# Tile pools that wait for the users of their own bytes: a four-layer perceiver in F32

## The chip, the cores and the metric

The kernel runs on one core of a Trainium2 chip (trn2). The metric is device time in microseconds for one launch. Five engines of the core have their own instruction streams: TensorE (PE in the profile, with its weight loads as PEld), VectorE (DVE), ScalarE (ACT), GpSimd (POOL) and SyncE (SP), which here mainly issues DMAs. [...]

## The reference

A perceiver of depth 4 on 128 latent tokens of width 256 (`x`), with a context of 12544 rows of width 192. Each layer adds three things to `x`, one after the other: cross-attention from the latents to the context, self-attention among the latents, and a feed-forward part with 8 experts.

- Cross-attention: `q = norm(x) Wq`, `k = ctx Wk`, `v = ctx Wv`, softmax over the context, then `Wo`. Layers 0 to 2 have 16 heads of 16; layer 1 also guards against keys that are not finite (it computes a mean of the values to put in their place); layer 3 has 16 heads of 64 and low-rank additions to its weights, the output's being `o_down` and `o_up`.
- Self-attention differs by layer: with a gate and scales (0), differential with lambda vectors and a norm (1), rotary (2), causal (3).
- Feed-forward: a router gives each token its experts; experts are gated or plain MLPs of inner width 1024.

All arithmetic that matters is F32.

## The kernel before

**Stages.** `run` (L1653) goes through the four layers in order; a layer is one cross-attention (`l0_xattn`, `xattn_biased` twice, `l3_xattn`), one self-attention (`l0_attn` to `l3_attn`) and one feed-forward (`l0_ffn` to `l3_ffn`). In the profile the cross-attentions take 0-564, 693-1217, 1372-1900 and 2010-2973 us; what lies between them are the joints, in which the self-attention and experts run (L0 564-686, L1 1217-1364, L2 1900-2007, L3 2974 to the end).

**Cross-attention.** `attend_twice` (L493, layers 0 to 2) reads the context twice in blocks of 512 rows: once for the highest score, once for exp and the weighted sum. The line numbers that come up are L102 (keys and values from the context), L538/L539 (scores and their maxima), L575/L581/L595 (scores again, exp, weighted values). At its end the accumulator is copied to `oT` (L649), transposed into `pair` (L652) and divided into `o`. `attend_once` (L660, layer 3) keeps scores in SBUF and goes over the context once. The queries lie in one tile `qz` with two halves, written by two DVE instructions (L295).

**Joints.** After layer 1's cross-attention `nan_guard` checks the keys' sums: `wide` and `many` are small constants made by DVE, then three products on TensorE, `ps<-wq,xT`, `ps<-wk,wide` with `ps<-row,many` (the row is the bias `bk`), and one with `wv`. After layer 3's cross-attention the output projection of `l3_xattn` opens the pool `out3` and a weights pool, loads `wo` and `od` (`o_down`), transposes `o3`, and multiplies: 16 matmuls with `od`, 16 with `wo`, then the row `bo` and the low-rank part `low`. `l3_attn` follows with `w_q`, `w_k`, `w_v`, `w_o`. A `softmax` (L466) is: DVE maximum and subtraction, ACT exp (L472), DVE sum, reciprocal and product.

**Loads.** `load_w` (L304, DMA at L311), `load_kv` (L322, L324), `load_row` (L335), `all_rows` (L341, a row broadcast to 128 partitions) and `load_b1` (L1597) put their DMAs on SP's queue, which issues in program order: a load that waits holds all loads behind it. The early context blocks of the next layer go over GpSimd's queue (L390, L392).

**Pools.** All tiles come from tile pools. Pools are stacked: a pool that is closed gives its range of SBUF (or its PSUM banks) back, and the next pool opened takes the same range. `const`, `wsmall`, `rows`, `xres`, `act`, `stat`, `ahead`, `broad` stay open all along; the pools of a stage (`x0`, `twice`, `a1`, `f3`, `once`, `out3`, `weights` and so on) open and close around it, and the PSUM pools are closed and opened anew by `psum` (L237) at each change of stage. Between a new pool's tile and what used the range before it, the framework puts semaphore waits; the scheduling of instructions on the engines' queues is otherwise the order of the program text.

## Time and profile before

| what | value |
|---|---|
| median of 3 runs | 3115.3 us (3112.16 to 3123.14) |
| profiled execution, its own time | 3119.43 us |
| its span | 3116.6 us |
| mean granted TensorE clock | 0.968 |
| busy: PE, DVE, ACT, POOL | 2966.8, 1955.4, 1469.2, 295.3 us |
| bytes read from HBM | 241.65 MB, 78 GB/s over the span |

The profile is of one execution; engines' busy times add up over instructions that overlap other engines' work. The chain is the sequence of work that ended last, followed back through what released each step. A timeline line gives start, length, engine, source line, operation with its output and inputs, and in brackets the engine's idle time before it and what ended that. The idle of an engine that is not the bottleneck costs nothing. Where TensorE works in 50 us stretches, it is busy for 35.0 us of 650-700, 43.4 of 1200-1250, 39.5 of 2950-3000 and 36.5 of 3000-3050; in the cross-attentions it is nearly full.

### The profile page before, as it was taken

How to read it: one execution, taken by the hardware profiler on the slowest of the kernel's cores; microseconds unless marked ns; L12 is line 12 of the kernel's file. 1: busy time of each engine (PE TensorE's matmuls, PEld its weight loads, DVE VectorE, ACT ScalarE, POOL GpSimd, SP SyncE). 2: the span in 40 equal slices, each digit the busy share in tenths (PEclk: the TensorE clock that was granted, in tenths of full speed). 3: DMA queues.
4: the chain of work that ended last, by engine and by line, in shares of the span. 5: the costliest groups of instructions: out<-in, count | busy, mean ns of one | idle time of the engine just before them, and what ended most of it. 6: DMA issues, size and time to landing. Idle time of an engine off the chain costs nothing.

```text
span 3116.6 us, 78239 instructions
## 1 busy us (share of the span) xinstructions
PE 2966.8 (95%) x35065; PEld 2248.6 (72%) x35065; DVE 1955.4 (63%) x2300; ACT 1469.2 (47%) x1869; POOL 295.3 (9%) x349
## 2 busy tenths in 40 slices
PE   8999999879999999899999999899999999999979
PEld 6677667535576576665676576489889889889858
DVE  7802850439997897769208603467777777777844
ACT  1187149411383185211572275256556565556511
POOL 6601630212000000110000001000000000000000
PEclk9999999989999998999999999899999999999979
DMA  5100210552002102441102106332323222322436
GB/s 134 52 18 26 72 39 3 188 204 58 25 3 62 53 14 75 126 130 50 31 13 70 46 3 203 118 86 81 87 78 87 80 85 81 87 82 84 121 109 204
DMA packets 165254, 246.83 MB, mean 79 GB/s; under 512 B 19853, under 2 KB 106831, under 8 KB 164920
## 3 DMA queue, kind: packets, MB, share of 16 engines
q1 hardware_dynamic: 160200, 227.67, 24.1%
q0 software_dynamic: 4608, 14.16, 1.4%
q8 instruction: 275, 4.51, 0.6%
q14 instruction: 59, 0.48, 0.1%
q10 hardware_dynamic: 112, 0.01, 0.0%
HBM read 241.65 MB, written 0.13 MB: 78 GB/s over the span
## 4 chain that ended last, share of the span: by engine, by line
PE 78%; DVE 11%; ACT 5%; issue 3%; DMA 2%; POOL 1%; SPq 0%; DVEq 0%; ACTq 0%; POOLq 0%
PE pair L102 20%; PE pair L538 9%; PE v L102 8%; PE pair L575 7%; PE pair L595 6%; PE sc L701 6%; PE acc L743 6%; PE ps L275 4%; DVE parts L539 4%; ACT e L581 3%; PE pair L567 2%; PE kv L102 2%; DVE e L289 2%; PE acc L275 2%; PE ps L1532 1%
## 5 line engine op out<-in xcount | busy, mean ns | idle before, releaser
L539 DVE TENSOR_REDUCE parts<-pair 128x2 f32<-128x1024 f32 x600 | 678.9, 1196 | 103.8 <-PE pair L538 103.7
L102 PE MATMUL pair<-ctxA,wk 128*128 128x256 f32 x1236 | 328.7, 399 | 1.4 <-ACT kT L193 1.1
L649 DVE COPY oT<-pair 128x256 f32<-128x256 f32 x6 | 2.5, 424 | 505.5 <-PE pair L595 505.5
L102 PEld LDWEIGHTS pair<-ctxA,wk 128*128 128x128 f32 x1236 | 217.2, 190 | 140.0 <-DVE parts L539 96.0
L538 PE MATMUL pair<-kT,qz 32*128 32x512 f32 (+1 forms) x1632 | 277.7, 612 | 9.3 <-DVE parts L539 8.9
L703 ACT COPY kept<-sc 128x1024 f32<-128x1024 f32 (+1 forms) x135 | 136.2, 1009 | 260.7 <-PE sc L701 260.6
L286 DVE TENSOR_TENSOR top<-top,kept 128x1024 f32<-128x1024 f32 (+2 forms) x145 | 169.1, 1169 | 135.0 <-ACT kept L703 133.8
L575 PE MATMUL pair<-qz,kT 32*128 32x256 f32 x3168 | 251.6, 374 | 0.0
L581 ACT ACTIVATE e<-pair,maskcol 128x512 f32<-128x512 f32 x392 | 237.0, 688 | 16.1 <-PE pair L575 14.9
L289 DVE SCALAR_TENSOR_TENSOR e<-pair,floor 128x1024 f32<-128x1024 f32 x196 | 230.3, 1218 | 7.1 <-PE pair L575 1.1
L587 ACT ACTIVATE e<-e 128x1024 f32<-128x1024 f32 x196 | 207.2, 1057 | 38.0 <-DVE e L289 30.4
L583 ACT ACTIVATE e<-pair 128x1024 f32<-128x1024 f32 x196 | 189.9, 1021 | 60.3 <-PE pair L575 60.3
L595 PE MATMUL pair<-e,v 128*17 128x128 f32 x6336 | 212.3, 274 | 2.0 <-ACT e L587 1.0
L575 PEld LDWEIGHTS pair<-qz,kT 32*128 32x128 f32 x3168 | 205.3, 187 | 10.8
L132 ACT ACTIVATE kT<-pair,bk 128x512 f32<-128x512 f32 (+1 forms) x68 | 45.9, 674 | 347.4 <-PE pair L102 323.5
L595 PEld LDWEIGHTS pair<-e,v 128*17 128x17 f32 x6336 | 156.6, 97 | 67.1 <-issue 42.5
L701 PE MATMUL sc<-qz,kT 64*128 64x128 f32 x2816 | 197.8, 279 | 0.0
L102 PEld LDWEIGHTS v<-wv,ctxA 128*128 128x128 f32 x1568 | 189.8, 192 | 6.4 <-issue 1.9
L567 PE MATMUL pair<-low,ones 32*128 32x512 bf16 x1176 | 190.4, 389 | 3.6 <-DVE low L558 3.1
L102 PE MATMUL v<-wv,ctxA 128*128 128x128 f32 x1568 | 193.1, 276 | 0.0
L102 PE MATMUL pair<-ctxB,wk 64*128 64x256 f32 x1236 | 188.3, 398 | 0.0
L701 PEld LDWEIGHTS sc<-qz,kT 64*128 64x128 f32 x2816 | 171.6, 187 | 13.0 <-issue 1.3
(425 smaller groups left out, 4866.2 us busy)
## 6 DMA issues: line engine op xcount, KB each, us to landing
ctxA<-in_ctxA SPq DMA_DIRECT2D x324, 256.0 KB
ctxB<-in_ctxB SPq DMA_DIRECT2D x339, 128.0 KB
w<-in_L_ffn_W SPq DMA_DIRECT2D x32, 1024.0 KB
ctxA<-in_ctxA POOLq DMA_DIRECT2D x36, 256.0 KB, 3.3
w<-in_L_ffn_w_gateT SPq DMA_DIRECT2D x8, 1024.0 KB
wu<-in_L_ffn_w_upT SPq DMA_DIRECT2D x8, 1024.0 KB
w<-in_L_ffn_w_downT SPq DMA_DIRECT2D x8, 1024.0 KB
w<-in_L_ffn_w1T SPq DMA_DIRECT2D x8, 1024.0 KB
```

The costliest lines, as they stand in the source:

```text
L102: self.nc.tensor.matmul(out, a, b, start=start and not low, stop=low == 1, skip_group_check=True)
L275: self.nc.tensor.matmul(out, lhsT, rhs, start=(i == 0), stop=(i == n - 1))
L289: self.nc.vector.scalar_tensor_tensor(out, a, s, b, op0, op1, **kw)
L538: nc.tensor.matmul(x[:, i, :n], qz[r, g, s, :], keys.kT(b)[r, :n], start=not masked, stop=True)
L539: nc.vector.tensor_reduce(parts[:, s, 2 * half : 2 * half + 2, b], x[:, :, :n], AX.X, ALU.max)
L567: nc.tensor.matmul(x[:, i, :], self.ones16[r, :], m[r, :], start=True, stop=False, skip_group_check=True)
L575: nc.tensor.matmul(at, kT[r, k], q, start=False, stop=True, skip_group_check=True)
L581: nc.scalar.activation(to[:, :, part], x[:, :, part], AF.Exp, bias=self.mask_col[:, c + j : c + j + 1])
L583: nc.scalar.activation(to, x, AF.Exp)
L587: nc.scalar.activation(to, to, AF.Exp)
L595: nc.tensor.matmul(acc[32 * t : 32 * t + 17, s, :P], v[:, c % 4 + j, 2 * t + s, :], es[t // 2][:, t % 2, j, s, :], start=c + j == 0, stop= ...
L701: nc.tensor.matmul(x[:, t, c : c + P], kT[r, c : c + P], qz[r, g, :], start=True, stop=True)
```

## The change

Every `tile_pool` call, at 21 places, gets `reuse_waits="tile"`. Before, the first use of a tile of a newly opened pool waits until all users of the released pools whose range the new pool lies on are done. After, a tile waits only for the users of the bytes on which it lies itself. Tiles keep their addresses, and the program's arithmetic, transfers and order of statements stay as they are. The diff is the same edit at each place; these carry the stages named above:

```diff
@@ Net.__init__ (const, wsmall, rows, xres, act, stat, ahead, broad)
-        pool = lambda name, bufs, **kw: ctx.enter_context(tc.tile_pool(name=name, bufs=bufs, **kw))
+        pool = lambda name, bufs, **kw: ctx.enter_context(tc.tile_pool(name=name, bufs=bufs, **kw, reuse_waits="tile"))
...
@@ psum: all PSUM pools
-            setattr(self, name, self.banks.enter_context(self.tc.tile_pool(name=name, bufs=bufs, space=PSUM)))
+            setattr(self, name, self.banks.enter_context(self.tc.tile_pool(name=name, bufs=bufs, space=PSUM, reuse_waits="tile")))
...
@@ large_weights
-        self.wp = self.tc.tile_pool(name="weights", bufs=bufs)
+        self.wp = self.tc.tile_pool(name="weights", bufs=bufs, reuse_waits="tile")
...
@@ attend_twice ("twice"), attend_once ("once") likewise
-        with self.tc.tile_pool(name="twice", bufs=2) as pool:
+        with self.tc.tile_pool(name="twice", bufs=2, reuse_waits="tile") as pool:
...
@@ xattn_biased (its own pool, "layer3", "guard"), l0_xattn ("x0", "layer3") likewise
-                with self.tc.tile_pool(name="guard", bufs=1) as own:
+                with self.tc.tile_pool(name="guard", bufs=1, reuse_waits="tile") as own:
...
@@ l3_xattn ("x3" and "out3")
-            with self.tc.tile_pool(name="out3", bufs=1) as last, self.large_weights() as self.wp:
+            with self.tc.tile_pool(name="out3", bufs=1, reuse_waits="tile") as last, self.large_weights() as self.wp:
...
@@ l0_attn to l3_attn ("a0" to "a3"), l0_ffn to l3_ffn ("f0" to "f3"), run ("narrow") likewise
-        with self.tc.tile_pool(name="a1", bufs=2) as pool:
+        with self.tc.tile_pool(name="a1", bufs=2, reuse_waits="tile") as pool:
```

More of the change, by code (lines that the diff above doesn't have):

```diff
@@ L666, in attend_once @@
         self.psum(ppr=1, pv=1, psc=1, pacc=1, pps=1)
-        with self.tc.tile_pool(name="once", bufs=2) as pool:
+        with self.tc.tile_pool(name="once", bufs=2, reuse_waits="tile") as pool:
             self.queue = self.nc.sync
@@ L862, in l0_xattn @@
         nc, d = self.nc, self.d
-        with self.tc.tile_pool(name="x0", bufs=2) as pool:
+        with self.tc.tile_pool(name="x0", bufs=2, reuse_waits="tile") as pool:
             wq = self.load_w(d["L0_xattn_Wq"], 2, D, "wq")
@@ L878, in l0_xattn @@
             o = self.ap.tile([P, D], F32, tag="o", name="o")
-            with self.tc.tile_pool(name="layer3", bufs=1) as other:
+            with self.tc.tile_pool(name="layer3", bufs=1, reuse_waits="tile") as other:
                 self.attend_twice(o, qz, keys, masked=True, between=self.prepare_l3(other))
@@ L897, in xattn_biased @@
         nc, d = self.nc, self.d
-        with self.tc.tile_pool(name=name, bufs=2) as pool:
+        with self.tc.tile_pool(name=name, bufs=2, reuse_waits="tile") as pool:
             xT = self.normed(x)
@@ L913, in xattn_biased @@
             else:
-                with self.tc.tile_pool(name="layer3", bufs=1) as other:
+                with self.tc.tile_pool(name="layer3", bufs=1, reuse_waits="tile") as other:
                     self.attend_twice(o, qz, keys, between=self.last_tokens_l3(other))
@@ L1062, in l3_xattn @@
         dims, rate = H * 64, self.rate
-        with self.tc.tile_pool(name="x3", bufs=2) as pool:
+        with self.tc.tile_pool(name="x3", bufs=2, reuse_waits="tile") as pool:
             xT = self.normed(x)
@@ L1136, in l0_attn @@
         nc, d = self.nc, self.d
-        with self.tc.tile_pool(name="a0", bufs=2) as pool:
+        with self.tc.tile_pool(name="a0", bufs=2, reuse_waits="tile") as pool:
             wide = pool.tile([P, 2 * P], F32, tag="wide", name="wide", bufs=1)
@@ L1316, in l2_attn @@
         nc, d = self.nc, self.d
-        with self.tc.tile_pool(name="a2", bufs=2) as pool:
+        with self.tc.tile_pool(name="a2", bufs=2, reuse_waits="tile") as pool:
             w = [self.load_w(d[f"L2_attn_{k}T"], 2, D, k) for k in ("wq", "wk", "wv", "wo")]
@@ L1347, in l3_attn @@
         dims = H * 64
-        with self.tc.tile_pool(name="a3", bufs=2) as pool:
+        with self.tc.tile_pool(name="a3", bufs=2, reuse_waits="tile") as pool:
             causal = pool.tile([P, P], F32, tag="causal", name="causal", bufs=1)
@@ L1601, in l0_ffn @@
         d = self.d
-        with self.tc.tile_pool(name="f0", bufs=2) as pool:
+        with self.tc.tile_pool(name="f0", bufs=2, reuse_waits="tile") as pool:
             xn = self.layernorm(x)
@@ L1609, in l1_ffn @@
         d = self.d
-        with self.tc.tile_pool(name="f1", bufs=2) as pool:
+        with self.tc.tile_pool(name="f1", bufs=2, reuse_waits="tile") as pool:
             xT = self.normed(x)
@@ L1625, in l2_ffn @@
         nc, d = self.nc, self.d
-        with self.tc.tile_pool(name="f2", bufs=2) as pool:
+        with self.tc.tile_pool(name="f2", bufs=2, reuse_waits="tile") as pool:
             b1 = pool.tile([NE, FF], F32, tag="b1", name="b1", bufs=1)
@@ L1637, in l3_ffn @@
         d = self.d
-        with self.tc.tile_pool(name="f3", bufs=2) as pool:
+        with self.tc.tile_pool(name="f3", bufs=2, reuse_waits="tile") as pool:
             xT = self.normed(x)
@@ L1668, in run @@
         made = []
-        narrow = self.tc.tile_pool(name="narrow", bufs=1)
+        narrow = self.tc.tile_pool(name="narrow", bufs=1, reuse_waits="tile")
         self.lw = narrow.__enter__()
```

## The prediction

> **What bounds the kernel now.** I read the page first: busy rows, then the chain that ended last.

> ```profile
> PE 2966.8 (95%) x35065; PEld 2248.6 (72%) x35065; DVE 1955.4 (63%) x2300; ACT 1469.2 (47%) x1869; POOL 295.3 (9%) x349
> ...
> PE 78%; DVE 11%; ACT 5%; issue 3%; DMA 2%; POOL 1%; SPq 0%; DVEq 0%; ACTq 0%; POOLq 0%
> ```

> TensorE is busy for 2966.8 of 3116.6 us, so all its idle time is 150 us, and no change that only removes waits can win more than that (plus whatever the clock gives back). Most of the chain is TensorE's own work. The idle time sits in the joints between stages (550-700, 1200-1300, 1900-2050, 2950-3050 us), which is also where pools are opened and closed. So the prediction is a list of joints, not a percentage.

> Next I read whom the SP queue waits for, because SP issues nearly every DMA, in program order. These waits look spectacular:

> ```profile
> SPq L1320 <- PE pair L652: 159.1, 1, 159.1
> SPq L341 <- DVE oT L649: 137.0, 1, 137.0
> SPq L311 <- PE pair L652: 129.1, 1, 129.1
> ```

> Three loads (L2 attention's `turns`, L1 attention's `norm`, L0 attention's `wqkv`) stand for 425 us in all, each held by the last user of a pool that has just closed. That is exactly the kind of wait that the change shortens. But SP is not on the chain (0%), so a shorter wait is worth only what somebody downstream loses to the late load. I read that from the timeline, joint by joint:

> ```profile
> 693.17 1.24 PE L538 MATMUL pair<-kv,qz 32*128 32x512 f32 x4 [0.79 <-DVE qz L295]
> ...
> 1218.02 1.10 PE L275 MATMUL ps<-wq,xT 128*128 128x256 f32 x4 [0.82 <-DVE many L936]
> ...
> 1219.77 0.25 SPq L335 DMA_DIRECT2D row<-in_L_xattn_bk  x1
> 1223.15 1.19 PE L275 MATMUL ps<-row,many 1*128 1x256 f32 x2 [2.35 <-DVE dot L286]
> ...
> 1244.07 1.28 ACT L472 ACT_TABLE_LOAD   x1
> 1250.10 0.63 ACT L472 ACTIVATE e<-e 128x512 f32<-128x512 f32 x1 [4.74 <-DVE e L286]
> 1256.75 0.42 DVE L281 COPY eT<-tr 128x256 f32<-128x256 f32 x1 [1.27 <-PE tr L1245]
> ...
> 2973.82 0.38 SPq L311 DMA_DIRECT2D wo<-in_L_xattn_Wo  x1
> 2979.57 1.65 PE L275 MATMUL ps<-wo,oT 128*128 128x256 f32 x3 [1.47 <-DMA wo<-in_L_xattn_Wo]
> 2985.85 0.25 SPq L335 DMA_DIRECT2D row<-in_L_ffn_b  x1
> 2986.33 0.38 SPq L311 DMA_DIRECT2D w_q<-in_L_attn_w_qT  x1
> 2991.48 0.76 PE L275 MATMUL ps<-xT,w_q 128*128 128x128 f32 x2 [2.53 <-DMA w_q<-in_L_attn_w_qT]
> ```

> The bracket is the engine's idle time before the line, with what ended it. These brackets of 0.8 to 2.5 us, not the 425 us, are the size of the prize.

> **The change, part by part.** Every tile keeps its place and every engine keeps its instruction order: PE 6329, DVE 1183, ACT 947, POOL 250 and SP 710 entries in the same sequence. No transfer and no arithmetic is added. Only wait operations differ (PE 3969 to 3961, DVE 2516 to 2499, ACT 2229 to 2226, SP 1831 to 1832, POOL 498 to 506). Most are gone because a tile lies on bytes that were free long ago; a few sit on another instruction of the same engine. A moved DMA passes nothing on SP or POOL: it can only go out as early as its predecessor.

> *Joints where TensorE itself was held.* At 693.17 and 1371.96 (the first scores of L1 and L2) TensorE had ended its own work 0.79 us earlier and waited for the second of two `qz` writes; now the first one, 2 us older, suffices. That is 2 x 0.7. At 1218.02 it waited 0.82 for the guard's memset of `many`, although `wq` and `xT` were there: 0.7. At 18 us and 564 us the same thing is worth 0.2 and 0.1. Sum 2.4.

> *The L1 guard's row (1219.77).* The freed `norm` load and the two lambda rows behind it leave SP at about 1172 instead of 1217, 45 us early. The loads behind them (`wq`, row `bk`, `wk`) keep their waits on TensorE, so they don't move, but row `bk` no longer queues behind three broadcasts. It was issued at 1219.77 and landed at 1223.01, 3.24 us; TensorE stood for 2.35 us before it (the bracket names `dot`, done at the same moment). With an empty queue what would it take? Other one-row loads of this trace land in about 1.4 us[...]. By the row, the stall shrinks to 0.5 and 1.9 is won; [...] if the queue was not the cause, 0. I take 1.3, since `wq` (256 KB) goes out 0.6 ahead of it in either kernel [...].

> *The L3 output projection (2973.82).* `wo` was held by the last write of `o3` and landed 5.7 us later, so TensorE, done with its own 16 `od` matmuls at 2978.10, stood for 1.47 us. Its bytes are now free at 2953.07 and SP's last load ahead of it leaves at 2958.3: it lands near 2964, ten microseconds before its use. The whole 1.47 goes; next in line is `low` (DVE, at 2978.14), which is used only by the last two matmuls. [...] I looked at the clock over its own grid of 3.41 us:

> ```profile
> 2973.21:2976.63 3.42, 2.62 (x12) 1.97 (x13) 1.18 (x3) 1.87 (x2) 0.00 (x0) 0.50 0.40 108
> 2976.63:2980.04 3.41, 1.94 (x8) 1.34 (x7) 0.34 (x1) 0.00 (x0) 0.00 (x0) 0.50 0.57 199
> 2980.04:2983.45 3.41, 3.41 (x9) 2.69 (x9) 0.00 (x0) 0.00 (x0) 0.00 (x0) 0.50 0.00 0
> 2983.45:2986.87 3.42, 2.80 (x12) 1.83 (x11) 0.55 (x2) 0.00 (x0) 0.49 (x2) 1.00 0.00 0
> ...
> 1232.50:1235.90 3.40, 3.40 (x13) 2.40 (x12) 1.61 (x6) 0.20 (x1) 0.00 (x0) 0.50 0.99 367
> 1235.90:1239.30 3.40, 2.88 (x15) 2.09 (x16) 0.57 (x2) 1.16 (x2) 1.07 (x2) 0.50 0.99 345
> ```

> (Stretch, length, then busy time of PE, PEld, DVE, ACT, POOL, and the granted clock.) The clock is 0.50 until the stretch 2980.04-2983.45 has been busy throughout, and 1.00 after it. [...] By that rule, once the idle 1.47 is gone the window before is full, the clock rises at 2980.04, and the 1.95 us of cold work left there takes half: 0.97 more. But the row 1232.50 speaks against the rule: 3.40 us busy, and the next stretch is still at 0.50. I take half, 0.5, with 0 and 1.0 as ends.

> *The next stall in the same chain (2986.33).* `w_q` loses its own wait (2973.74 instead of 2986.26), which alone would remove up to 2.1 of the 2.53 us bracket. It is behind L3 feed-forward's row `b2` on SP, though, and that one still waits for the `bo` matmul (2985.83) to release a row buffer. So `w_q` leaves only 0.24 earlier relative to its surroundings: 0.2. The bracket at 2991.48 stays.

> *Waits that appear.* Two ACT table loads of 1.28 us (L472 at 1244.07 and at 1916.87) ran while ACT idled; the wait for DVE now sits on the table load and no longer on the `exp` after it, so each `exp` starts 1.28 later (1250.10 to about 1251.4; 1920.90 to about 1922.2). Behind each are DVE's reduction and normalisation, then the transposes. The trace bounds the price: 2 x 1.28 = 2.6 if nothing absorbs it, 0 if DVE's own gaps do (1.27 before `eT` at 1256.75, 1.04 at 1925.21). The gaps are nearly as long as the shift: 0.2. Another such move (L1470 at 1297.35) meets an ACT that is busy anyway.

> *Costed at nothing.* `wqkv` of L0 attention goes out 3.9 earlier (560.06), but lands 2.5 before its use and is paced by `xT` (569.95). `bv` at 669 and 1364, `turns` (used 11 us later, and `w1` behind it on SP keeps its wait until 1901.56), `qu` (TensorE busy until 2011.02), both `b1` loads, POOL's memsets for `v`, `before` and `causal` (the last waited 1020.7 us): each is needed well after it was already there. If that cover were gone, each would cost under 0.5.

> *Sum.* 2.4 + 1.3 + 1.5 + 0.5 + 0.2 - 0.2 = 5.7 us off the profiled execution, which took 3119.4 us (span 3116.6, 2.8 around it). It stands 4.1 above the median of 3115.3; I take the gain off the median: 3109.6. The ends of the terms give 1 to 8.

> **The rivals.** *More than the brackets (30%).* The granted clock averages 0.968; at levels 0.5 and 1 that is 3116.6 x 0.032 x 2, some 199 us at half speed. The stretch 1222.2-1242.7 is one block of it, TensorE busy there for 17.6 of 20.5 us. It went cold after 1218.8-1222.2, in which TensorE was busy for only 2.0 of 3.4 us, partly by the two stalls that go. If it stays warm, up to half of 17.6 could go, but DVE and the expert weights pace that stretch too, so 3 to 6: 3104 to 3107, with another window or two elsewhere 3100. Against it: TensorE's next stalls there are not touched.

> *Nothing (12%).* The bytes are free but each load's next obstacle (its predecessor on SP, its row buffer) is as late as the old one, as for `w_q`; or the tiles lie on the last-used bytes after all. Only the 0.7s remain: 3113 to 3116.

> *Slower (7%): the clock's phase.* All work after 1218 slides by 2 to 5 us over a grid of 3.41 us that doesn't slide with it. [...] From four more cold windows than now (6.8) the gain is eaten; seven cost 11.9 and end at 3121. For it: dozens of windows lie in the joints. Against: the sliding warms as many as it cools, and less idle time makes windows fuller.

> **How the numbers follow.** Forecast 51%, 3109.6, its own range 3105 to 3114. About 0.3% (9.3 us) is what a measurement can tell from no change: 3106. The forecast lies on the near side; a fifth of its chance lies beyond, with most of the "more" case: faster 0.36. Slower keeps 0.06, since part of that rival ends within 9.3 us. The same: 0.58. The range leaves out a tenth on either side: 3099 to 3117.

> **What would show it.** Right: brackets under 0.2 at the first scores of L1 and L2 and at the guard's first product; `norm` issued near 1172; `wo` issued near 2958 and no DMA bracket at its matmul; row `b2` still just ahead of `w_q`, with 2 us or more idle before `w_q`; the two table loads directly ahead of their `exp`. Wrong: `w_q` leaving ten microseconds early; the clock at 1.00 through 1222-1243; a new bracket over 1 us in front of a TensorE line where none stands now; a shift of `exp` that is still there at the end of L1 or L2 attention.

## The result and the profile after

The changed kernel took 3109.7 us (median of 6 executions, 3103.8 to 3111.4), the kernel before 3123.6 us beside it (6 executions): a ratio of 0.996, 95% interval 0.9941 to 0.998. A later repetition (11 executions against 25) gave 3112.1 and 3121.1, ratio 0.9974, interval 0.9966 to 0.9983. So the change is worth 8 to 12 us. The forecast named 3109.6 us and a gain of 5.7. That the time agrees to 0.1 us is luck: the kernel before ran 8 us slower beside it than the median of 3115.3 from which the gain was taken (6 us slower in the later repetition). The gain itself is one and a half to two times the forecast.

The page of the changed kernel, busy rows and the chain that ended last:

```profile
PE 2958.3 (95%) x35065; PEld 2247.1 (72%) x35065; DVE 1954.4 (63%) x2300; ACT 1470.4 (47%) x1869; POOL 296.2 (10%) x349
...
PE 80%; DVE 11%; ACT 5%; issue 2%; DMA 1%; POOL 1%; SPq 0%; DVEq 0%; ACTq 0%; POOLq 0%
```

The span fell by 14.5 us (3116.6 to 3102.1), TensorE's busy time by 8.5, although every matmul is still there. The mean granted clock is 0.973 where it was 0.968; that is the first trace of the part that the forecast had missed. This profile is of the fastest of the six executions, though. The repetition's profile has a span of 3111.5 us and TensorE busy for 2966.4, hardly less than before, so what one profile says of the clock has to be set against many executions, as is done below.

SP's waits, whom it waited for, with total, number and longest:

```profile
SPq L1320 <- PE pair L575: 155.4, 1, 155.4
SPq L311 <- PE pair L575: 125.1, 1, 125.1
...
SPq L341 <- PE pair L595: 93.4, 1, 93.4
```

Two of the three spectacular waits are hardly shorter: 159.1 and 129.1 became 155.4 and 125.1. The third, `norm`, fell from 137.0 to 93.4. They end on an earlier matmul of the same cross-attention. Nobody on the chain needed those loads; `norm` matters only for the small load that stood behind it in the queue, row `bk`.

The timeline at the places that the prediction showed:

```profile
690.40 1.23 PE L538 MATMUL pair<-kv,qz 32*128 32x512 f32 x3
...
1169.93 0.33 SPq L341 DMA_DIRECT2D norm<-in_L_attn_norm_w  x1
...
1215.65 1.03 PE L275 MATMUL ps<-wq,xT 128*128 128x256 f32 x4
...
1217.34 0.24 SPq L335 DMA_DIRECT2D row<-in_L_xattn_bk  x1
1219.15 0.67 PE L275 MATMUL ps<-row,many 1*128 1x256 f32 x2 [0.78 <-DMA row<-in_L_xattn_bk]
...
1244.52 1.28 ACT L472 ACT_TABLE_LOAD   x1 [5.61 <-DVE e L286]
1245.81 0.63 ACT L472 ACTIVATE e<-e 128x512 f32<-128x512 f32 x1
1251.61 0.42 DVE L281 COPY eT<-tr 128x256 f32<-128x256 f32 x1 [0.82 <-PE tr L1245]
...
2946.89 0.43 SPq L311 DMA_DIRECT2D wo<-in_L_xattn_Wo  x1
2963.68 3.62 PE L275 MATMUL ps<-oT,od 128*32 128x128 f32 x16
2967.23 4.36 PE L275 MATMUL ps<-wo,oT 128*128 128x256 f32 x16
2972.25 0.24 SPq L335 DMA_DIRECT2D row<-in_L_ffn_b  x1
2972.58 0.38 SPq L311 DMA_DIRECT2D w_q<-in_L_attn_w_qT  x1
2977.52 1.19 PE L275 MATMUL ps<-xT,w_q 128*128 128x128 f32 x4 [2.17 <-DMA w_q<-in_L_attn_w_qT]
```

The brackets of 0.79, 0.82 and 1.47 are gone, the one before `row,many` fell from 2.35 to 0.78, `wo` goes out 20 us ahead of its use, and `w_q` still leaves right behind row `b2` with 2.17 us of idle time after it.

To see where the rest came from, I cut each profiled execution at the same instructions: a joint runs from the last `oT` copy of a cross-attention (L649) to the first maximum of the next (L539). L2's ends instead at the square root in the layer norm that opens L3's cross-attention (L434). The last three rows are cut at the last reciprocal of L3's cross-attention (L779), at the square root in L3 attention's layer norm (L434), and where the input of the feed-forward's first sigmoid (L1472) is ready. In brackets stands the time of each at a granted clock of 0.5 (cold time, below), in us, summed from the clock's records.

| | before | after | after, repeated |
|---|---|---|---|
| joint L0 to L1 | 132.3 (29.5) | 124.3 (11.3) | 129.4 (23.3) |
| joint L1 to L2 | 158.0 (36.0) | 153.0 (30.9) | 153.5 (31.0) |
| joint L2 to L3 | 108.8 (23.9) | 104.0 (13.7) | 107.2 (20.5) |
| L3 tail to L3 attention's norm | 14.7 (10.2) | 11.6 (6.2) | 11.6 (6.1) |
| L3 attention to L3 feed-forward | 57.7 (30.7) | 56.9 (30.7) | 56.9 (30.7) |
| L3 feed-forward to the end | 71.3 (0.1) | 71.2 (0.4) | 71.2 (0.5) |

The rows add up to 21.8 us less in the first profile and 13.0 in the repetition. What the table leaves out, the start and the cross-attentions, took 2573.7 us before, 2581.1 after and 2581.7 in the repetition, so 7 to 8 us of that go back. Experiments 3 and 6, which leave nearly all waits there as they were, have 2579.5 and 2578.3, so the profile before stands at the low end of a spread, and what the change itself does to these stages is not shown. The joint after layer 0, to which the forecast had given 0.8 us, gained 8 in one execution and 3 in the other, and its cold time (time at clock 0.5) explains the difference. Two questions follow: is the clock's part caused by the change, and by which pools?

### The profile page after: what moved, and what is told of

It is laid out like the page before. It is cut to its first block, busy times and chain, and to the rows that moved or that the text cites. A ratio compares the mean times of both kernels' runs of the same rounds, so it can differ in the third digit from the quotient of the medians.

```text
span 3102.1 us, 78224 instructions
## 1 busy us (share of the span) xinstructions
PE 2958.3 (95%) x35065; PEld 2247.1 (72%) x35065; DVE 1954.4 (63%) x2300; ACT 1470.4 (47%) x1869; POOL 296.2 (10%) x349
## 4 chain that ended last, share of the span: by engine, by line
PE 80%; DVE 11%; ACT 5%; issue 2%; DMA 1%; POOL 1%; SPq 0%; DVEq 0%; ACTq 0%; POOLq 0%
PE pair L102 20%; PE pair L538 10%; PE pair L575 9%; PE pair L595 8%; PE v L102 7%; PE sc L701 6%; PE acc L743 5%; PE ps L275 4%; DVE parts L539 4%; ACT e L581 3%; PE pair L567 3%; PE kv L102 2%; PE acc L275 2%; PE ps L1532 1%; PE pair L537 1%
## 5 line engine op out<-in xcount | busy, mean ns | idle before, releaser
L539 DVE TENSOR_REDUCE parts<-pair 128x2 f32<-128x1024 f32 x600 | 679.1, 1197 | 103.7 <-PE pair L538 103.6
L649 DVE COPY oT<-pair 128x256 f32<-128x256 f32 x6 | 2.5, 424 | 508.4 <-PE pair L595 508.4
L538 PE MATMUL pair<-kT,qz 32*128 32x512 f32 (+1 forms) x1632 | 277.7, 615 | 9.8 <-DVE parts L539 9.6
L286 DVE TENSOR_TENSOR top<-top,kept 128x1024 f32<-128x1024 f32 (+2 forms) x145 | 169.1, 1169 | 133.9 <-ACT kept L703 132.6
L587 ACT ACTIVATE e<-e 128x1024 f32<-128x1024 f32 x196 | 207.2, 1057 | 38.5 <-DVE e L289 30.9
```

Source lines behind the costliest of these rows:

```text
L538: nc.tensor.matmul(x[:, i, :n], qz[r, g, s, :], keys.kT(b)[r, :n], start=not masked, stop=True)
L539: nc.vector.tensor_reduce(parts[:, s, 2 * half : 2 * half + 2, b], x[:, :, :n], AX.X, ALU.max)
L587: nc.scalar.activation(to, to, AF.Exp)
```

## The experiments

**1. PSUM pools alone.** All 20 edits of SBUF pools are taken back; this line stays:

```diff
-            setattr(self, name, self.banks.enter_context(self.tc.tile_pool(name=name, bufs=bufs, space=PSUM)))
+            setattr(self, name, self.banks.enter_context(self.tc.tile_pool(name=name, bufs=bufs, space=PSUM, reuse_waits="tile")))
```

> Only the PSUM pools (the one line in psum) wait by tile; every SBUF pool as before. Sum of terms: the three 0.7-0.8 brackets of TensorE at the first scores of L1 and L2 and at the guard's first product go (2.1), and 0.3 at 18 and 564 us: 2.4 us faster than before (ratio 0.9992). The big SP waits (137, 159, 129 us) and the 1.47 before wo stay. Rival (the clock is chance): time and cold time differ from before by up to 8 us either way whatever is freed, and only the brackets tell. Rival (freed SP queue makes the gain): nothing here, same as before.

Measured: 3117.4 us against 3122.1 (22 and 59 executions), ratio 0.9984, interval 0.9974 to 0.9995. Twice the expected 2.4, and the mean clock is higher (0.9684 against 0.9668). L0's joint fell to 125.7 us (12.6 cold) from 132.3 (29.5); L1's only to 156.8. The guard shows why the second stayed (timeline of this kernel):

```profile
1214.70 1.03 PE L275 MATMUL ps<-wq,xT 128*128 128x256 f32 x4
...
1220.68 1.19 PE L275 MATMUL ps<-row,many 1*128 1x256 f32 x2 [3.27 <-DMA row<-in_L_xattn_bk]
```

The 0.82 before `wq,xT` is gone, and the wait for row `bk` grew from 2.35 to 3.27: TensorE arrived earlier at a row that didn't. From the transposes of `oT` to the `row,many` product it takes 6.25 us, before 6.39. Here the PSUM part is worth next to nothing without the SBUF part, which takes the row out from behind the three broadcasts.

**2. SBUF pools alone.** The counterpart: the 20 SBUF edits stay, `psum` is as before.

> All SBUF pools wait by tile, the PSUM pools as before. Sum of terms: out-projection 2.0 to 2.8, row bk 1.3, others 0: 3.5 to 4 us faster than before (0.9988). Rival (freed SP queue): nearly the whole 14 us of the change, 0.996, with L0's joint (567 to 692 us) 5 us or more shorter than in before. Rival (chance of the clock): L0's joint is as much shorter or longer as its cold time says, and not the same from run to run.

Measured: 3118.2 us against 3122.1 (22 and 59 executions), ratio 0.9993, interval 0.9978 to 1.0007: the medians differ by as much as expected, but no change lies within the interval. L0's joint is 133.3 us, as before, so the freed SP queue does not shorten it; the L3 tail is 11.9 and the guard 4.87. The theory that the freed queue makes the whole gain falls.

**3. The L3 output projection alone.**

```diff
-            with self.tc.tile_pool(name="out3", bufs=1) as last, self.large_weights() as self.wp:
+            with self.tc.tile_pool(name="out3", bufs=1, reuse_waits="tile") as last, self.large_weights(reuse_waits="tile") as self.wp:
```

> Only the pool out3 and the weights pool opened with it, of the L3 output projection, wait by tile. wo is issued some 15 us ahead of its use; the bracket of 1.47 goes; the chain from the first od matmul to the residual add shrinks by 2.0 (half of the clock's term) to 2.8 (as the trace after had it): 0.9992. Nothing changes ahead of it but chance.

Measured: 3120.4 us against 3122.1, ratio 0.9992, interval 0.9979 to 1.0004: the size expected, not separable from no change by the times. The trace has it: the L3 tail takes 12.1 us (6.8 cold) instead of 14.7 (10.2), and `wo` follows `od` at once:

```profile
2982.98 3.62 PE L275 MATMUL ps<-oT,od 128*32 128x128 f32 x16
2986.53 3.73 PE L275 MATMUL ps<-wo,oT 128*128 128x256 f32 x11
```

**4. `w_q` out from behind row `b2`.** The changed kernel, with the feed-forward's bias rows of layer 3 on GpSimd's queue:

```diff
-            b2 = self.load_row(b2, D) if b2 is not None else None
+            b2 = self.load_row(b2, D, queue=nc.gpsimd if act == "silu" else None) if b2 is not None else None
```

> The changed kernel, and L3 feed-forward's bias rows (b2) are loaded over GpSimd's queue, so that SP no longer holds w_q, w_k, w_v and w_o behind row b2. Own theory: w_q leaves when the last write of o3 is done (about 9 us earlier), lands before xT, its bracket of 2.2 falls under 0.3; the projections that follow are bound by w_k only if it lands later than 6 us after: 2 us faster than the changed kernel, up to 4 with the clock (3106 to 3108 where the changed kernel has 3109.7). Rival: w_q's own wait was not what the trace says, the bracket stays, no change.

Measured: 3112.9 us against 3122.1 (6 and 59 executions), ratio 0.9959, interval 0.9944 to 0.9975: not faster than the changed kernel (3109.7, and 3112.1 in the repetition), where 2 us had been expected. `w_q` left 12.5 us ahead of its first matmul (4.9 in the changed kernel) and its bracket fell to 0.46, which is ACT's copy of `xT` (the queue's line, then the engine's):

```profile
2976.21 0.38 SPq L311 DMA_DIRECT2D w_q<-in_L_attn_w_qT  x1
```

```profile
2988.70 5.46 PE L275 MATMUL ps<-xT,w_q 128*128 128x128 f32 x32 [0.46 <-ACT xT L283]
```

L3 attention took 55.3 us instead of 56.9, but its cold time grew from 30.7 to 32.9 and the feed-forward to the end took 72.1 instead of 71.2. So the reading of the SP queue was right, but of the 2 us that it was to bring only 0.7 are left at the end of this profile, and none shows in the times.

**5. The changed kernel again.** Same file, for more executions.

> The changed kernel once more, for more executions and a second profile. Own theory now: the gain has a direct part (waits removed, about 3 us at equal clock) and a part through the clock[...]. Then the lower cold time is a property of the kernel: mean clock near 0.971 again (0.967 before), time near 3109, L0's joint near 124 us in the profile. Rival (the first executions were lucky): clock back to 0.967 to 0.969, time 3115 to 3119, and L0's joint back to 130 or more.

Measured: 3112.1 us, ratio 0.9974 (0.9966 to 0.9983), mean clock 0.9695 over 11 executions (0.9676 for the 25 of before beside it). Neither theory's numbers: L0's joint is 129.4, between 124 and 132. The clock is higher than before's in both sets, by 0.0019 here and by 0.0047 in the first set against before's 59 executions, so part of the first result was luck and part was not.

**6. PSUM pools of one joint.** The kernel before, with waits by tile for the PSUM pools of the third call of `psum` alone, those that open after layer 0's cross-attention:

```diff
+        self.laid = getattr(self, "laid", 0) + 1
+        kw = {"reuse_waits": "tile"} if self.laid == 3 else {}
```

> The kernel before, with waits by tile only for the four PSUM pools that open at the end of layer 0's cross-attention. Own theory: the 0.3 to 1.0 us that TensorE loses at the first transposes and at one later copy are gone, the block of two cold windows 48 us into the joint goes with them, and L0's joint falls from 132 to about 126 us while all other joints stay: 3 to 5 us faster than before (0.9985 to 0.999). Rival (the shorter L0 joint in the profiles with PSUM waits by tile is chance): 132 us as before, no change.

Measured: 3116.3 us against 3121.1 (14 and 25 executions), ratio 0.999, interval 0.9979 to 1.0001: the size expected, but the times alone do not quite separate it from no change. The profiles do. L0's joint is 126.5 us (13.3 cold), as expected; L1's joint is 158.5 and L3's tail 14.4, untouched. Over all profiles the joint takes 132.3, 133.3 and 134.9 us with the old PSUM waits (before, experiments 2 and 3) and 124.3 to 129.5 in the seven with the new ones (after and its repetition, 1, 4, 6, and 7 and 8 below). What tips is one window of the clock. First before, over three steps of the clock's own 3.41 us grid (stretch, length, busy PE, PEld, DVE, ACT, POOL, granted clock, DMA):

```profile
604.37:607.78 3.41, 2.15 (x22) 1.78 (x20) 3.41 (x11) 1.21 (x3) 1.51 (x2) 1.00 0.29 79
607.78:611.20 3.42, 1.63 (x8) 1.14 (x8) 2.68 (x8) 1.24 (x1) 1.44 (x3) 1.00 0.11 38
611.20:614.61 3.41, 3.41 (x9) 1.91 (x8) 0.13 (x1) 0.00 (x0) 1.35 (x3) 0.50 0.40 121
```

and the same place in experiment 6:

```profile
606.85:610.27 3.42, 2.16 (x21) 1.76 (x19) 3.32 (x12) 1.53 (x3) 1.51 (x2) 1.00 0.23 74
610.27:613.68 3.41, 2.38 (x12) 1.53 (x10) 1.70 (x4) 0.91 (x1) 1.54 (x3) 1.00 0.13 38
613.68:617.09 3.41, 3.08 (x23) 2.15 (x22) 1.76 (x6) 0.93 (x3) 1.02 (x3) 1.00 0.74 208
```

In the middle window TensorE is busy for 1.63 of 3.42 us before, and the clock is at 0.5 for the next two windows; with 2.38 it stays at 1.00. TensorE's wait at the transposes of `o` in that window, before and in experiment 6:

```profile
610.26 0.44 PE L447 MATMUL tr<-ident,o 128*128 128x128 f32 x2 [1.79 <-DVE o L286]
```

```profile
611.67 0.44 PE L449 MATMUL tr<-ident,o 128*128 128x128 f32 x2 [1.03 <-DVE o L288]
```

A shift of under a microsecond turned a window that was 48% busy into one 70% busy, and saved two cold windows.

The other profiles bear this out. A cold block begins 48 us into the joint in all three with the old PSUM waits (it lasts 6.8, 13.7 and 6.8 us) and in none of the seven with the new ones. Chance in where the clock's windows fall is not the reason: the joint begins 2.7 to 3.2 us after a window's start in all ten profiles. The cold windows later in the joint are not as steady. Experiment 6 loses some of them too, the repetition keeps them, and that makes the difference between joints of 126 and of 129 us.

**7. Filling the gaps of layer 3.** The changed kernel, with matmuls that nobody reads placed where TensorE waits (52 in all; the expectation counts them as 44):

```diff
+    def fill(self, out, n, rhs=None):
+        for _ in range(n):
+            self.nc.tensor.matmul(out, self.ones, self.ones if rhs is None else rhs, start=True, stop=True)
...
+        if hd == 64:
+            self.fill(t[:, 0, :], 5, self.lately)
```

> The changed kernel, with 44 matmuls that nobody reads (F32, 128 x 128, ones times data just ready), in the gaps of layer 3's joint where TensorE waits: before both layer norms' transposes, before w_q, before each head group's transposes, before the last reduction of the cross-attention. They do no work of the reference. Own theory: TensorE's cold time between L3 attention's layer norm and L3 feed-forward's first sigmoid (30.7 us in every profile so far) falls to 10 or so, and the stage from 57 us to 52 to 54; the clock term is then a cause, not a companion: 3 to 5 us faster than the changed kernel. Rival (the cold clock there only fills time that DVE and ACT need anyway): the cold time falls and the stage stays within 1 us of 57, or grows by what the fillers take.

Measured: 3102.7 us against 3121.1 (6 and 25 executions), ratio 0.9942, interval 0.9929 to 0.9955: the best kernel here, some 9 us below the changed one's 3112.1 of the same set. Its profile is of the fastest of the six (3093.1). There the cold time from L3 attention's norm to the feed-forward's first sigmoid fell from 30.7 to 3.4 us and the stage from 56.9 to 49.1, more than expected. First the changed kernel, then this one, in the head groups of L3 attention:

```profile
2999.28:3002.70 3.42, 2.10 (x10) 1.78 (x8) 2.01 (x6) 0.00 (x0) 0.00 (x0) 0.50 0.00 0
3002.70:3006.11 3.41, 2.16 (x9) 1.76 (x10) 2.26 (x4) 1.11 (x2) 0.44 (x2) 0.50 0.00 0
3006.11:3009.52 3.41, 1.64 (x9) 1.45 (x8) 2.43 (x6) 0.13 (x1) 0.00 (x0) 0.50 0.00 0
```

```profile
2999.69:3003.10 3.41, 2.30 (x19) 2.11 (x19) 2.39 (x6) 0.98 (x2) 0.00 (x0) 1.00 0.00 0
3003.10:3006.51 3.41, 2.18 (x16) 1.70 (x16) 2.65 (x6) 0.63 (x1) 0.00 (x0) 1.00 0.00 0
3006.51:3009.93 3.42, 3.08 (x21) 2.64 (x22) 0.88 (x2) 0.59 (x1) 0.00 (x0) 1.00 0.00 0
```

More matmuls, less time: TensorE's busy time per window is about equal, but at full clock it does twice as many (56 against 28 in the three, fillers included). The clock is thus a cause of time in that stage and not something that merely fills DVE's time.

**8. Fillers and early `w_q`.** Experiments 4 and 7 together.

> e7 with L3 feed-forward's bias rows on GpSimd's queue as in e4. Own theory: w_q's bracket of 2.2 us goes as in e4 (stage 2 us shorter) and the fillers keep the clock; 2 us faster than e7. Rival: the earlier weights only move the cold window, as in e4, where the stage fell by 2 and its cold time grew by 2; no faster than e7.

Measured: 3106.5 us against 3121.1 (5 and 25 executions), ratio 0.9951, interval 0.9937 to 0.9964: not faster than 7, and the times overlap, so the 2 us of the expectation are not there. In its profile the stage took 53.6 us with 17.1 cold: the head groups went cold once, at 3015.6, and stayed so for 17 us. That fits the rival, that the earlier weights only move the cold window; but this profile is of the slowest of the five executions and that of 7 of the fastest of its six, so one pair of profiles does not show it.

## Why the prediction was right and where it was short

*The direct terms held.* First scores of L1 and L2: both brackets of 0.79 are gone (forecast 0.7 each). Guard: from the transposes of `oT` to the `row,many` product 6.39 us before (1216.76 to 1223.15), 3.77 after (1215.38 to 1219.15) and 4.17 in the repetition: 2.6 and 2.2 won where 2.0 stood. The queue was the cause of the late row: from issue to landing row `bk` took 3.2 to 3.8 us in the four profiles where the broadcasts leave just ahead of it (before, experiments 1, 3 and 6) and 1.7 to 2.2 in the six others. The prediction's 1.4 holds only for some of the other rows: in the profile before, eight landed after 1.2 to 1.9 us and fourteen after 2.0 to 5.0. The 1.3 of the sum was my estimate between the two ends 1.9 and 0; row `bk` landed 1.6 us sooner after its issue (3.24 before, 1.68 after), and the stall shrank by 1.6. Output projection: from `od` to the residual add 11.81 before (2974.48 to 2986.29), 9.01 after (2963.68 to 2972.69): 2.8 where 2.0 stood. Here one full window was followed by 1.00, as at 2980.04 before, and my half was too careful. After the change (stretch, length, busy PE, PEld, DVE, ACT, POOL, granted clock, DMA):

```profile
2965.15:2968.56 3.41, 3.41 (x14) 2.57 (x12) 0.34 (x1) 0.00 (x0) 0.00 (x0) 0.50 0.02 5
2968.56:2971.97 3.41, 3.41 (x16) 2.73 (x16) 0.00 (x0) 0.00 (x0) 0.00 (x0) 1.00 0.00 0
```

The clock rises in the midst of `wo` (2967.23 to 2971.59), at 2968.56. The cold block there lasts 6.8 us in all seven profiles in which `wo` is freed and 10.2 in the three in which it is not. `w_q`: bracket 2.53 to 2.17, forecast 0.2.

Table loads: the first `exp` is 1.3 us later relative to its surroundings (the reduction behind it moved back by 1.34 in the first profile after, for both layers), and 0.85 to 0.95 of it came back by the second transposes' copy or reduction: 0.4 a layer, forecast 0.2 for both. In the repetition layer 1 lost nothing. All loads that were costed at nothing cost and gained nothing that a bracket shows.

*The step that failed is the clock's term.* I gave it 0.5 us, for one window at `wo`, and said of the rest that the sliding "warms as many as it cools". The runs say otherwise. In the 59 executions of the kernel before in the first set, time and mean granted clock go together (correlation -0.90): the 7 with a clock under 0.9645 took 3132.0 us in the mean, the 11 above 0.9685 took 3116.1. From a line through them, 0.001 of clock is worth 2.3 us. The 17 executions of the changed kernel have a mean clock of 0.9702 and take 3110.3 us; before has 0.9668 and 0.9676 in its two sets, 3122.1 and 3120.9. So by this line 6 to 8 us of the 10.5 to 11.8 between these means go with the clock. What is left at equal clock is some 4 us, and a fit with one slope for all kernels gives 3.6 and 5.4 for the two sets of the changed kernel, each with a standard error of about 1, which agrees with the forecast's 5.2 without its clock term. A line through executions does not say which causes which; that the clock costs time is shown by experiment 7.

Experiment 6 shows removed waits that bought clock: one window went from 1.63 to 2.38 us busy of 3.42, and two cold windows behind it are gone. Nearly all removed waits stand in joints, where TensorE was busy for 436.6 of 518.6 us before (2521.4 of 2579.0 in the cross-attentions). That less idle time keeps more windows at 1.00 than the sliding takes from it is my reading of the sum; it does not hold for each wait, as experiment 4 shows, where one went and the cold time grew. So the rival "more than the brackets" came nearest, but not by its own place: the block 1222.2 to 1242.7 shrank only from 20.5 to 13.6 us cold after and to 17.1 in the repetition. (In experiment 4, the same kernel up to there, it shrank to 3.4, and the joint still took 154.8 us.) In the first profile most came from L0's joint, 18.2 of 30.4 us of cold time, and no rival had named that.

*Do the parts add?* PSUM alone gave 0.9984, SBUF alone 0.9993, which makes 0.9977; together they gave 0.996 and 0.9974, and both intervals hold 0.9977. So for the whole kernel the times don't show that the parts fail to add. At the guard they do fail: 0.1 us won with PSUM alone, 1.5 with SBUF alone, 2.1 to 2.6 in the five profiles with both. The earlier product only waits longer for a row that the other half frees (experiment 1).

*Left open.* L2's joint goes with its cold time: over the ten profiles it takes 108.8 or 108.9 us with 23.9 us cold, 106.9 to 107.5 with 20.5, 105.7 with 17.1 and 104.0 with 13.7, which is half a microsecond for each one cold, or some 1.6 for a step of 3.41 (the "slower" rival's 6.8 for four cold windows was an estimate of that size). So nothing is left there for a freed load as such; which removed wait moved the clock there was not tried apart. Why experiment 8 falls into a cold block that 7 avoids is seen only as a window of the profile, once each.

## What to carry to other kernels

Read the brackets of the bounding engine, not the totals of the DMA queue: of 425 us of SP waits only one mattered, by the small load queued behind it (a stall of 2.35 us fell to 0.8 and 1.2), and 0.8 to 2.4 us in front of TensorE carried the direct gain. Then look where the clock stands at 0.5: in layer 0's joint, under a microsecond less idle in a window that was 48% busy saved two cold windows of 3.41 us, and 52 matmuls in gaps brought as much as the 21 edits of pools (3121.1 to 3112.1, then to 3102.7). Compare such kernels at equal clock as well as by medians, or the spread of the clock (16 us here between the cold and the warm executions of one kernel) hides effects of 3 to 5 us.
